# Starting the slabs of the second attention 0.8 ticks later, and the last sums four ticks later

## The chip, the cores and the metric

The kernel runs on one core of a Trainium2 chip. The metric is the device time of one execution in microseconds. The time before is the median of three runs, 2865.06 us (2863.92 to 2869.85). About 0.2% is what such a measurement can tell from no change.

## The reference

The input `x` has 128 graphs of 64 nodes with 768 features, and `adj` is a mask of 64 x 64 for each graph. There are two layers. Each computes an attention over the nodes of a graph under the mask, adds its input and normalises. The first layer (12 heads of 64) takes its scores from tanh of the hidden features, and mixes its result with its input through a gate. The second (6 heads of 128) is ordinary attention with queries, keys, values and an output matrix:

```python
q = _heads(seq_inputs @ Wq + bq)
k = _heads(seq_inputs @ Wk + bk)
v = _heads(seq_inputs @ Wv + bv)
scores = jnp.einsum('bhqd,bhkd->bhqk', q, k) / np.sqrt(HEAD_SIZE)
bias = jnp.where(graph_mask, 0.0, NEG)[:, None]
probs = jax.nn.softmax(scores + bias, axis=-1)
ctx = jnp.einsum('bhqk,bhkd->bhqd', probs, v)
ctx = ctx.transpose(0, 2, 1, 3).reshape(seq_inputs.shape[0], seq_inputs.shape[1], H)
return ctx @ Wf + bf
```

All is float32. The change touches only the second layer.

## The kernel before

The 8192 tokens are 64 tiles of 128 tokens (two graphs each). The first phase treats them in pairs of tiles and ends by about 1440 us. The second treats them in 16 quads of four tiles. Matrix products are made by schemes with fewer multiplications: a product of 2 x 2 blocks takes 7 products of sums of blocks (`TURNS`), and the output matrix, 2 x 3 blocks by 3 x 3, takes 15 (`FIFTEEN`). TensorE therefore waits for sums that VectorE (DVE) or GpSimd (POOL) make, and its results are read out by DVE or ScalarE (ACT).

A quad runs through three steps, f = 0, 1, 2, each for two heads (f and f + 3). A step has these parts:

- `queries` and `keys`: seven products each, in `by_feature` (L442). The readers of their results are given by `p1` to `p7`: P1 and P2 go to ACT (L422 and L425), the others to DVE (L418, L428, L431, L434). The results stand in `zone`, in one buffer for queries and one for keys. The five PSUM banks of the pool `dense` are used in turn by all these products.
- `slab(Q, f)`: the scores (`s_ps`, L991), with mask and maximum on DVE (L1001, L1005), subtraction (L1007), exponential on ACT (L1009), sum and division on DVE (L1012 to L1016). Then the weights are turned: ACT sorts them into halves (L1030), SP issues a transposing DMA (L1031), ACT sorts them back in two copies (L1035). TensorE multiplies them with the values (`c_ps`, L1047). ACT copies this out in two halves (L1061), two transposing DMAs follow on SP (L1062), and four ACT copies (L1069) put the result into `cT`. In the last quad's f = 2, TensorE turns the weights and no DMA is used. Just after `c_ps` of f = 2, the mask and the values of the next quad are loaded (`load`: L970, and eight DMAs at L980).
- `output(before, i)`, at f = 1 and f = 2: the 15 products (L1135) for two tiles (i = 0, then 1) of the quad before. DVE adds each result to a row tile `y` (L1148).

The sums of the output's scheme are made by `operands` (L1102 on DVE; in the last quad's second pair also L1100 on POOL). Rows are loaded by `rows_of` (L1113 on SP, then POOL adds a bias, L1118), and `normed` closes a tile: statistics on DVE (L363 to L368), a power on POOL (L370, L371), the scaling on ACT (L1161) and the store on SP (L1163). There are four `y` buffers; a load into one waits until the store from it has landed. In the keys of f = 2, each operand block of the next quad is loaded as soon as its product has been issued (L397).

Every engine executes its instructions in the order in which the program issues them. That order is written by `Beat`, a clock that exists only while the program is built. A query, key or value product advances it by one tick, an output product by 2/3. `start` puts a line of steps (a generator) on this clock: its first step comes `after + 0.7` ticks from now, and each `yield n` puts the next step n ticks later. The reader of a product comes 1.5 ticks after it. Nothing waits for ticks on the chip: they decide only what stands before what in each engine's queue.

```python
def step(time):
    wait = next(line, None)
    if wait is not None:
        self.at(time + wait, lambda: step(time + wait), order)
time = self.now + after + 0.7
self.at(time, lambda: step(time), order)
```

The slab of a step is started when its keys have been issued. Its scores thus come 1.7 ticks after the keys, `c_ps` 12 ticks after the scores, the first copies into `cT` 18 and the second 19 ticks after them. Since 2/3 is added many times over, steps whose times nearly agree can change places from one quad to the next.

After the last quad, `output` runs twice more. The sums for its second pair of tiles are started 5 ticks (and 0.7) after those of the first.

Of the kernel before, what the change touches and what calls it, by code (L numbers as in the profile page):

```python
# [208 lines left out]
def two_layers(  # L209
# [23 lines left out]
    n_quads = n_tiles // 4  # L233
    n_pairs = n_tiles // 2
    beat = Beat()
# [5 lines left out]
    def sb(pool, shape, tag, name, bufs=None, dtype=F32):  # L241
        return pool.tile(shape, dtype, tag=tag, name=name, bufs=bufs)
# [140 lines left out]
    def in_zone(at, *shape):  # L383
        size = math.prod(shape)
        letters = " ".join("abc"[: len(shape)])
        sizes = dict(zip("abc", shape))
        return zone[:, at : at + size].rearrange(f"p ({letters}) -> p {letters}", **sizes)
# [4 lines left out]
    def load_block(q, k):  # L392

        at = PLACES[k] * KH
        t = in_zone(IN_ZONE[k] * D, KH, 2, P)
        for i in range(2):
            nc.sync.dma_start(t[:, :, i, :], ops_there[q][:, i, at : at + KH, :])  # L397
        return t.rearrange("p c i t -> p c (i t)")

    def queries(q, f, blocks, part):  # L400
        quads[q]["qT"] = in_zone(7 * KH * 2 * P, 2, 4 * P)
        by_feature(f"q_{q}_{f}_", blocks, ready["wq_sb"], f, bq_sb, quads[q]["qT"], part)

    def keys(q, f, blocks, part, then=None):
        quads[q]["kT"] = in_zone((7 * KH + 4) * 2 * P, 2, 4 * P)
        by_feature(f"k_{q}_{f}_", blocks, ready["wk_sb"], f, bk_sb, quads[q]["kT"], part, then)
# [500 lines left out]
    def phase_b(pb, ps_b):  # L907
# [166 lines left out]
        def operands(Q, i):  # L1074

            while not Q.get("done"):
                yield 1
            c = Q["c"][i]
            A = [c[:, :, k, m] for m in range(2) for k in range(3)]

            last = Q["q"] + 1 == n_quads and i == 1
            s = in_zone(0, 11, 2, P) if last else sb(pb, [P, 11, 2, P], "sc", f"sc_{Q['q']}_{i}", 1)
            of = Q["ob", i] = {f"A{k}": a for k, a in enumerate(A)}
            sums = (
                ("3", 1.0, "A0", "A2", ALU.subtract),
                ("12", -1.0, "3", "A3", ALU.subtract),
                ("2", 1.0, "A5", "A4", ALU.subtract),
                ("11", 1.0, "2", "3", ALU.subtract),
                ("14", 1.0, "A0", "A3", ALU.add),
                ("7", -1.0, "A1", "A3", ALU.subtract),  # L1090
                ("0", 1.0, "A1", "A4", ALU.add),
                ("10", 1.0, "0", "A5", ALU.subtract),
                ("5", 1.0, "A0", "A1", ALU.subtract),
                ("1", 1.0, "10", "A2", ALU.subtract),
                ("6", 1.0, "A3", "A4", ALU.subtract),
            )
            for k, (name, sign, a, b, op) in enumerate(sums):
                of[name] = s[:, k]
                if last and sign == 1.0:
                    nc.gpsimd.tensor_tensor(s[:, k], of[a], of[b], op)  # L1100
                else:
                    nc.vector.scalar_tensor_tensor(s[:, k], of[a], sign, of[b], ALU.mult, op)  # L1102
                yield 1

        def rows_of(Q, i):
            q = Q["q"]

            while "bias" not in ready or q and not all(quads[q - 1].get(("out", i, k)) for k in range(2)):
                yield 1
            for k in range(2):  # L1110
                t = 4 * q + 2 * k + i
                y = sb(pb, [P, D], "y", f"y_{t}", 4)
                nc.sync.dma_start(y, x1_there[t])  # L1113
                Q["y", i, k] = y
            yield 2
            for k in range(2):
                y = Q["y", i, k]
                nc.gpsimd.tensor_tensor(y, y, bf_sb, ALU.add)  # L1118
                yield 1

        def output(Q, i):
            q, of = Q["q"], Q["ob", i]
            y = [Q["y", i, k] for k in range(2)]
            sums = {}
            left = [sum(b // 3 == k for *_, to in FIFTEEN for _, b in to) for k in range(2)]
            for at, xb, wb, to in FIFTEEN:
                beat.until(lambda: xb in of)
                begun = at in sums
                if not begun:
                    sums[at] = sb(dense[0], [P, BANK], "dense", f"o_{q}_{i}_{at}")[:, 0:THIRD]  # L1130
                ps = sums[at]

                def emit():
                    for c in range(2):
                        nc.tensor.matmul(  # L1135
                            ps,
                            lhsT=of[xb][:, c, :],
                            rhs=wf_sb[:, wb, c, :],
                            start=(c == 0 and not begun),
                            stop=(c == 1),  # L1140
                            skip_group_check=True,
                        )

                def read(ps=ps, to=to):
                    for sign, b in to:
                        k, n = divmod(b, 3)
                        part_of = y[k][:, n * THIRD : (n + 1) * THIRD]
                        nc.vector.tensor_tensor(part_of, part_of, ps, ALU.add if sign > 0 else ALU.subtract)  # L1148
                        left[k] -= 1
                        if not left[k]:  # L1150
                            beat.start(normed(y[k], 4 * q + 2 * k + i), 0)

                beat.product(emit, read, 2 / 3)
# [12 lines left out]
        Q, before = quads[0], None  # L1166

        def at_place(q, f):

            return (None, 0, 1)[f]  # L1170

        load(Q)
        for q in range(n_quads + 1):
            for f in range(3):
                if f == 2 and q < n_quads:
                    beat.start(rows_of(Q, 0))
                if f == 0 and before:
                    beat.start(rows_of(before, 1))
                if before and at_place(q, f) is not None and (q < n_quads or f == 1):
                    beat.start(operands(before, at_place(q, f)))  # L1180
                    if q == n_quads and f == 1:
                        beat.start(operands(before, 1), 5)
                if q < n_quads and (q or f):
                    queries(q, f, blocks, part)
                if q < n_quads:
                    then = None
                    if f == 2 and q + 1 < n_quads:
                        then = lambda xb: blocks.update({xb: load_block(q + 1, xb)})
                    if q or f:
                        keys(q, f, blocks, part, then)  # L1190
                    beat.start(slab(Q, f), 1)
                i = at_place(q, f)
                if before and i is not None:
                    beat.until(lambda: ("ob", i) in before)
                    output(before, i)
            before, Q = Q, quads.get(q + 1)
        beat.drain()

    with (
        tc.tile_pool(name="pb", bufs=1) as pb,  # L1200
        tc.tile_pool(name="ps_b", bufs=1, space=PSUM) as ps_b,
        tc.tile_pool(name="dense_b", bufs=5, space=PSUM) as dense_b,
        tc.manual_schedule(),
    ):
        dense[:] = [dense_b]
        phase_b(pb, ps_b)
# [47 lines left out]
```

## Time and profile before

| what | value |
|---|---|
| median of three runs | 2865.06 us |
| the profiled execution, its own time | 2868.3 us |
| its span | 2866.4 us |
| granted TensorE clock, mean | 0.994 |
| TensorE busy | 2804.1 us, 98% of the span |
| VectorE busy | 2039.1 us, 71% |
| ScalarE busy | 1305.3 us, 46% |
| GpSimd busy | 1067.2 us, 37% |
| first scores of the second layer | 1441.8 us |
| last c_ps turned by DMA | 2792.85 us |

The profiled execution runs about 2 us longer than its span, and about 3 us longer than the median. In the views below, a row of waits names the engine and line that waited, and what it waited for, with the total, the number of times and the longest. A row of the timeline has its start, its length, the engine, the line, the instruction and how many were merged; `[t <- X]` is idle time ahead of it and what ended it. SPq is the queue of SP, and its time is that of issuing a DMA, including what it waits for in the course of that, not that of the transfer. In a table of windows the third last number is the granted TensorE clock, followed by the share of the DMA engines and GB/s.

### The profile page before, as it was taken

Reading aid. Unit: us, or ns where it says so; the run is one execution under the profiler, and the core shown is the slowest. Engines: PE = TensorE matmul, PEld = TensorE weight load, DVE = VectorE, ACT = ScalarE, POOL = GpSimd, SP = SyncE. Lnnn points to the kernel's source line nnn. Section 1 sums busy time; section 2 is a strip of 40 time slices with the busy share of each in tenths; the row PEclk is TensorE's granted clock in tenths of the full one; section 3 lists DMA queues with packets and bytes.
Section 4 is the critical chain, followed back from the end, with each engine's and each line's share of the span. In section 5 each row is a group of like instructions: output and inputs, shape, how many; then the busy total and the mean of one; then the engine's idle time right before and its main releaser. Section 6 shows DMA issues by size and latency. Waiting matters only on the chain.

```text
span 2866.4 us, 43840 instructions
## 1 busy us (share of the span) xinstructions
PE 2804.1 (98%) x16168; PEld 2038.1 (71%) x16168; DVE 2039.1 (71%) x4103; ACT 1305.3 (46%) x1562; POOL 1067.2 (37%) x938
## 2 busy tenths in 40 slices
PE   7899999999999999999899999999999999999998
PEld 4455555555555555555588888888888888888886
DVE  6888888888888888888636555565555655556556
ACT  2655655665665665665423333333333333333331
POOL 6656656666665665665421101101011110110102
PEclk9999999999999999999999999999999999999999
DMA  6666666666666666667764445534355343554532
GB/s 205 152 175 170 175 168 169 179 165 170 182 163 172 179 165 170 186 160 193 195 156 116 106 100 131 135 87 117 86 130 135 90 120 84 127 135 94 128 82 63
DMA packets 627014, 409.61 MB, mean 143 GB/s; under 512 B 440176, under 2 KB 573040, under 8 KB 626800
## 3 DMA queue, kind: packets, MB, share of 16 engines
q1 hardware_dynamic: 626800, 406.81, 55.2%
q8 instruction: 128, 2.10, 0.3%
q14 instruction: 86, 0.70, 0.1%
HBM read 186.69 MB, written 119.93 MB: 107 GB/s over the span
## 4 chain that ended last, share of the span: by engine, by line
PE 89%; DMA 4%; DVE 2%; SPq 1%; ACT 1%; issue 1%; POOL 0%; POOLq 0%; ACTq 0%; DVEq 0%
PE v L346 15%; PE o L1135 15%; PE h L346 14%; PE g L346 14%; PE q L442 14%; PE k L442 12%; PE f_all L742 2%; PE s_ps L991 2%; PE c_ps L1047 2%; DMA out<-y 2%; DMA sT<-parts 2%; SPq L980 1%; ACT cT L1069 0%; PE bias_ps L951 0%; DMA s<-parts 0%
## 5 line engine op out<-in xcount | busy, mean ns | idle before, releaser
L370 POOL TENSOR_TENSOR rs<-rs,power 128x1 f32<-128x1 f32 x128 | 73.9, 577 | 1079.4 <-DVE rs L368 1079.4
L346 PE MATMUL h<-w,zone 128*128 128x384 f32 x1320 | 446.2, 494 | 21.7 <-ACT h L533 12.5
L442 PE MATMUL q<-zone,w 128*128 128x256 f32 x2016 | 461.6, 384 | 3.8 <-issue 1.2
L346 PE MATMUL g<-w,zone 128*128 128x384 f32 x1320 | 441.3, 489 | 4.4 <-DVE gate L587 3.3
L442 PE MATMUL k<-zone,w 128*128 128x256 f32 x2016 | 443.2, 379 | 0.9 <-ACT k_u L422 0.9
L442 PEld LDWEIGHTS q<-zone,w 128*128 128x128 f32 x2016 | 381.2, 191 | 63.5 <-issue 8.4
L442 PEld LDWEIGHTS k<-zone,w 128*128 128x128 f32 x2016 | 382.9, 190 | 53.4 <-ACT k_u L422 1.3
L346 PEld LDWEIGHTS h<-w,zone 128*128 128x128 f32 x1320 | 250.7, 192 | 194.6 <-ACT h L533 13.7
L346 PEld LDWEIGHTS g<-w,zone 128*128 128x128 f32 x1320 | 247.5, 190 | 176.4 <-DVE gate L587 12.8
L1135 PE MATMUL o<-w,sc 128*128 128x256 f32 x1364 | 326.7, 384 | 4.7 <-DVE sc L1102 4.7
L1148 DVE TENSOR_TENSOR y<-y,o 128x256 f32<-128x256 f32 x512 | 206.7, 415 | 126.7 <-PE o L1135 120.1
L1135 PEld LDWEIGHTS o<-w,sc 128*128 128x128 f32 x1364 | 256.1, 191 | 43.8 <-DVE sc L1102 6.0
L346 PE MATMUL v<-w,x_sums 128*128 128x384 f32 x768 | 258.5, 486 | 1.7 <-DVE x_sums L315 1.7
L1118 POOL TENSOR_TENSOR y<-y,bf_sb 128x768 f32<-128x768 f32 x64 | 118.4, 1865 | 342.4 <-DMA y<-x_there 313.9
L662 POOL TENSOR_TENSOR bc_e<-th_d,w_dst_sb 128x768 f32<-128x768 f32 x64 | 120.0, 1875 | 287.2 <-ACT th_d L557 267.6
L346 PEld LDWEIGHTS v<-w,x_sums 128*128 128x128 f32 x768 | 145.7, 190 | 104.0 <-DVE x_sums L315 3.0
L1161 ACT ACTIVATE y<-y,rs 128x768 f32<-128x768 f32 x64 | 65.7, 1026 | 157.8 <-POOL rs L371 157.8
L657 POOL TENSOR_SCALAR zone<-zone 128x768 f32<-128x768 f32 x64 | 137.3, 2146 | 0.0
L1009 ACT ACTIVATE s<-s 128x512 f32<-128x512 f32 x48 | 30.1, 626 | 226.2 <-DVE s L1007 226.2
L1102 DVE SCALAR_TENSOR_TENSOR sc<-cT 128x256 f32<-128x256 f32 x217 | 113.9, 525 | 22.9 <-ACT cT L1069 22.8
L650 ACT ACTIVATE gate<-gate 128x768 f32<-128x768 f32 x64 | 53.9, 843 | 166.8 <-DVE gate L593 118.5
L733 ACT COPY bc_e<-th_d 128x1536 uint16<-128x1536 uint16 x64 | 123.2, 1926 | 13.2 <-DMA th_d<-bc_e 13.2
(162 smaller groups left out, 4625.1 us busy)
## 6 DMA issues: line engine op xcount, KB each, us to landing
zone<-ops_there SPq DMA_DIRECT2D x224, 192.0 KB, 4.4
zone<-in_xT SPq DMA_DIRECT2D x32, 768.0 KB, 6.2
zone<-in_x SPq DMA_DIRECT2D x64, 384.0 KB, 3.9
bc_e<-there SPq DMA_DIRECT2D x128, 192.0 KB, 3.4
x_there<-mix SPq DMA_DIRECT2D x64, 384.0 KB, 4.2
ops_there<-x_sums SPq DMA_DIRECT2D x32, 768.0 KB, 3.3
v_there<-v SPq DMA_DIRECT2D x128, 192.0 KB, 2.6
v<-v_there SPq DMA_DIRECT2D x128, 192.0 KB, 3.9
```

The source lines that it names most:

```text
L346: nc.tensor.matmul(ps, lhsT=blocks[xb][:, c, :], rhs=w[:, wb, c, :], start=(c == 0 and to not in begun), stop=(c == KH - 1), skip_group_ch ...
L370: nc.gpsimd.tensor_tensor(rs[:, 0:1], rs[:, 0:1], power, ALU.pow)
L442: nc.tensor.matmul(ps, lhsT=w[:, wb, c, f * P : (f + 1) * P], rhs=blocks[xb][:, c, :], start=(c == 0 and to not in begun), stop=(c == KH - 1),
L657: nc.gpsimd.tensor_scalar(xs, xs, 1.0, None, ALU.add)
L662: nc.gpsimd.tensor_tensor(bc, th, w_dst_sb, ALU.mult)
L733: nc.scalar.copy(halves(e), by_halves(d))
L742: nc.tensor.matmul(f_all[b * N : (b + 1) * N, at : at + E0 + 1], lhsT=e[rows, hd // 2 * P + b * N : hd // 2 * P + (b + 1) * N], rhs=(h[row ...
L1102: nc.vector.scalar_tensor_tensor(s[:, k], of[a], sign, of[b], ALU.mult, op)
L1118: nc.gpsimd.tensor_tensor(y, y, bf_sb, ALU.add)
L1135: nc.tensor.matmul(ps, lhsT=of[xb][:, c, :], rhs=wf_sb[:, wb, c, :], start=(c == 0 and not begun), stop=(c == 1), skip_group_check=True,)
L1148: nc.vector.tensor_tensor(part_of, part_of, ps, ALU.add if sign > 0 else ALU.subtract)
L1161: nc.scalar.activation(y, y, AF.Identity, bias=rs[:, 1:2], scale=rs[:, 0:1])
```

## The change

Two numbers in the loop of the second phase change. The slab of a step starts 1.8 ticks (and 0.7) after its keys have been issued instead of 1; the very last slab (last quad, f = 2) keeps its 1. The sums for the very last pair of tiles start 9 ticks (and 0.7) after instead of 5.

```diff
                 if before and at_place(q, f) is not None and (q < n_quads or f == 1):
                     beat.start(operands(before, at_place(q, f)))
                     if q == n_quads and f == 1:
-                        beat.start(operands(before, 1), 5)
+                        beat.start(operands(before, 1), 9)
                 if q < n_quads and (q or f):
                     queries(q, f, blocks, part)
...
                     if q or f:
                         keys(q, f, blocks, part, then)
-                    beat.start(slab(Q, f), 1)
+                    beat.start(slab(Q, f), 1 if q + 1 == n_quads and f == 2 else 1.8)
```

No instruction is added or removed. What changes is the place of a slab's steps among the products and their readers in the queues of TensorE, DVE, ACT and SP, and of the last sums in those of DVE and POOL.

## The prediction

> **What bounds the kernel now.** I read the page first, then the waits of TensorE from 1350 us on (the second attention), then the chain that ended last, then SP's and ACT's timelines around its bends.
>
> ```profile
> PE 2804.1 (98%) x16168; PEld 2038.1 (71%) x16168; DVE 2039.1 (71%) x4103; ACT 1305.3 (46%) x1562; POOL 1067.2 (37%) x938
> ```
>
> TensorE is busy in 98% of the span, and the change adds and removes no matmul. It can only alter the idle 62 us, and the clock. The waits in the second attention:
>
> ```profile
> engine line waited for: us in total, times, longest us
> PE s_ps L991 <- ACT zone L425: 9.3, 11, 2.2
> ...
> PE o L1135 <- DVE sc L1102: 4.7, 3, 2.1
> ```
>
> All eleven 9.3 us stand at the scores of f=0, once a group of four tiles: 0.47 us at 1689, then 1.24, 2.22, 0.33, 0.31, 0.91, 0.40, 0.79, 0.91, 0.47, 1.23 from 1955 to 2755. The chain shows what is late in the last of them:
>
> ```profile
> 2743.85 0.33 ACT k_u L422
> 2744.18 4.19 DMA out<-y
> ...
> 2748.84 4.71 DMA sT<-parts
> ...
> 2754.26 0.75 ACT cT L1069
> 2755.01 0.34 ACT zone L425
> ...
> 2755.39 1.15 PE s_ps L991 x32
> ```
>
> Read upwards: the scores need a key block that ACT finishes at L425; ahead of L425 in ACT's order stand the copies L1069 of the previous group's f=2 slab; they need its second transpose; that stands on SP behind a load of y, which waits until a store of out has landed and freed its buffer. The same stretch of SP, in this late group and in an early one:
>
> ```profile
> 2737.84 6.25 SPq L980 DMA_DIRECT2D v<-v_there  x8
> 2744.18 0.55 SPq L1163 DMA_DIRECT2D out<-y  x1
> 2744.81 1.39 SPq L1062 DMA_TRANSPOSE s<-parts  x1
> 2746.25 2.49 SPq L1113 DMA_DIRECT2D y<-x_there  x2
> 2748.84 1.24 SPq L1062 DMA_TRANSPOSE sT<-parts  x1
> ```
> ```profile
> 1585.10 5.19 SPq L980 DMA_DIRECT2D v<-v_there  x8
> 1590.35 1.07 SPq L1113 DMA_DIRECT2D y<-x_there  x2
> 1591.51 1.27 SPq L1062 DMA_TRANSPOSE s<-parts  x1
> 1592.87 3.34 SPq L1062 DMA_TRANSPOSE sT<-parts  x1
> ```
>
> Early groups (quads 1 to 4) store both out tiles before the v loads, so their y loads wait for nothing (1.07 us, not 2.49); from quad 5 on the order is the other one. This gives a natural measure. From one f=2 c_ps (L1047) to the next the timeline has 88.07, 88.61, 88.06 and 88.08 us early; later 89.14, 91.79, 88.22, 88.20. From 1584.21 to 2737.33 are 13 periods in 1153.12 us; at 88.06 they would take 1144.78. The excess is 8.34 us, and the last wait (1.23) comes after it: 9.57 us in all.
>
> [...] alone (L1031 at 2764.42) its reader starts 4.39 us later; behind v and y loads (1591.51) 5.84. [...] after the 2.22 us wait the granted clock is 0.50 in 2047 to 2049, which is why that period lost 3.7; and in the tail:
>
> ```profile
> 2826.00:2828.00 2.00, 2.00 (x6) 1.57 (x5) 1.46 (x6) 0.03 (x1) 0.98 (x3) 0.50 0.50 197
> ```
>
> [...] sums at L1102 take 0.42, but 1.76 at 2835.20 while POOL runs L1118, and 0.94 and 0.96 beside POOL's L1100.
>
> **The change, part by part.** (1) The later start moves every step of a slab 0.8 ticks down. A product is one tick, 6 matmul records or 1.29 us (7 take 9.06); an output product is 0.86. In the built order the scores of f=0 stand after three products of the next queries, not two; c_ps of f=2 after five, not four; c_ps of f=0 after the first output product, not before it; scores of f=1 and f=2 after four output products, not three. Count of instructions, DMAs and bytes is the same.
>
> (2) SP's order from quad 5 on becomes the early one in every group: out, out, mask, eight v, two y, two transposes. Behind f=1 both y loads also go ahead of both transposes, as quads 1 to 5 have them today; the zone loads follow either way 9.0 to 9.3 us after the first out store.
>
> (3) What late groups then wait: c_ps f=2 and the scores shift by the same 1.29 us, so twelve products still lie between (16.77 us when undisturbed). L425 must begin 0.51 before the scores. In the early order it begins 15.66, 16.79, 16.02 and 15.31 us after c_ps: slack 0.60, -0.53, 0.24, 0.95. In the late order 17.58, 18.54, 16.65, 16.64, 17.24. In quads 1 to 5 of the changed kernel L425 also passes ahead of the second pair of copies (1.27 us less), so no wait; in quads 6 to 14 it does not, and one in four of the early order's sizes would wait 0.54: 9 x 0.13 = 1.2 us remain. So -9.6 + 1.2 = -8.4.
>
> (4) Covers of the moved steps. The product that now precedes the scores needs a PSUM bank last read by DVE (third product of the keys, read at 2750.3, needed at 2754.2): hidden. The weights' copy before f=0's c_ps: L1030 moves behind the next k_u on ACT (ready 2764.9 in the old clock), transpose 4.4, two copies 1.4: ready 2771.9, c_ps due at 2773.1: 1.2 us slack (2.0 today). For f=1 and f=2 a y normalisation (1.03) now stands between the two weight copies of L1035; today both end 1.0 to 1.2 before c_ps. In f=1 the second copy would end at 2793.5, its half of c_ps due at 2794.6: 1.1 slack. Early groups already run this order (1581.65, 1582.62, 1583.55 on ACT) with a c_ps that does not wait. Queued behind these copies are L425 of the queries, due 6 us later at the bank, and the c_ps reads. Cost 0; if the slack were gone, each tenth of a us would count 45 times. Bounds: -1 to +3 us.
>
> (5) The tail: sums of the last pair start four ticks later. DVE's one at 2836.88 ("12" of the last pair, 0.94 long) goes behind "6" of the pair before; POOL's first ("3") goes behind both L1118. TensorE's 2.10 us wait at 2839.43 ends with DVE's "10", which began at 2838.41. Without the 0.94 it would start about 2837.6 and last 0.96 again, as POOL now does three sums there: product "10" at 2838.6, 0.8 us earlier. POOL's remaining sums, behind the powers at 2845.4 and 2847.5, run to about 2852 at 0.73 each; "14" is needed at 2850.8, "10" at 2852.4, "6" at 2855.8: covered. The 1.73 and 0.90 waits before stay, and the half clock with them. -0.8, bounds -1.5 to +1.5.
>
> Sum: -8.4 + 0 - 0.8 = -9.2. The profiled execution took 2868.3 (span 2866.4); it becomes 2859.1. The median of the three is 2865.06, 3.2 below it; taking the same difference from that: 2855.9.
>
> **The rivals.** *A: the wait stays under a new name.* With the y loads (768 KB) ahead of both, the first transpose lands later (13.1, 14.3, 12.9, 12.8 us after c_ps early, against 11.1 to 12.5 in late groups); if late groups sit where the 14.3 sits, each of nine waits 0.54 and the clock now and then halves. For: the second quad did. Against: three of four have slack. Then 9.6 - 4.9 + 0.8 saved less one clock loss of 1.5: 2861.
>
> *B: nothing.* The waits of 0.3 to 1.2 in late groups depend on where DMA landings fall (out stores also load the queues); shifted by the same 1.29 as their consumer they keep their size, and only the tail's 0.8 is saved: 2864. Against: the order that delays the second transpose is gone from every group.
>
> *C, slower: the weights' copies become the bound.* The y normalisation between the two L1035 copies waits for a power from POOL; in early groups ACT waits 4.1 us for one of these. If it comes more than 1.1 us late at f=1 or f=2, c_ps waits, 30 times. At 0.6 us each, 18 us lost, less 9: 2874. It decides from 1.1 us of lateness; the row of L370 waits for DVE's sums of squares, whose place beside the output products does not move. Against it also the early groups.
>
> *D: the tail starves.* If POOL's sums ran at the 0.8 to 0.95 they take beside DVE, "10" would be 0.5 late at most; inside the bounds.
>
> **How the numbers follow.** Forecast (2852 to 2859): 0.62. A: 0.14. B: 0.13. C: 0.11. Bounds of parts 4 and 5, and a spread of the before's own runs of 1 below to 5 above their median, widen the forecast to 2850; A and B are taken in up to 2865; C is left out. About 0.2% (5.7 us, so 2859.3) is what a measurement here tells from no change: the forecast and a third of A are beyond it, so faster 0.69 after a little for the forecast's own upper edge and parts of A; within: the rest of A and B and a few of the forecast, 0.20; slower 0.11.
>
> **What would show it.** In the changed kernel's waits "s_ps <- ACT zone" should fall from 9.3 to about 1 us; periods between f=2 c_ps should be 88.0 to 88.6 throughout; on SP no y load after v should take over 1.5 us; L425 should begin 15.3 to 16.8 after c_ps; TensorE's last "o <- DVE sc" wait should be about 1.3, not 2.1. The forecast is wrong if c_ps shows waits for ACT L1035 or L1161, if the bank of the third product waits, or if periods keep 88.3 or more.

## The result, and the profile after

The changed kernel takes 2859.33 us (median of 8 runs, 2854.74 to 2859.91) against 2868.86 us for the kernel before, run beside it (8 runs, 2863.88 to 2873.95). The ratio is 0.9962, with a 95% interval of 0.9952 to 0.9971: faster by 9.5 us. The prediction was a fall of 9.2 us, to 2855.9 from a median of 2865.06; the kernel before, run again, lies 3.8 us above that median, so it is the falls that compare. The profiled execution of the changed kernel took 2859.59 us, with a span of 2857.3; before, 2868.3 and 2866.4.

The page of the changed kernel, engines:

```profile
PE 2803.1 (98%) x16168; PEld 2039.0 (71%) x16168; DVE 2042.6 (71%) x4103; ACT 1309.1 (46%) x1562; POOL 1063.8 (37%) x938
```

TensorE's busy time is 1.0 us less than it was (2804.1). So 8.1 of the 9.1 us of span are idle time that has gone. TensorE's waits in the second attention of the changed kernel (total, times, longest):

```profile
engine line waited for: us in total, times, longest us
...
PE o L1135 <- DVE sc L1102: 5.0, 3, 2.3
...
PE s_ps L991 <- ACT zone L425: 1.5, 3, 0.6
...
PE q L442 <- DVE zone L428: 1.2, 1, 1.2
PE q L442 <- ACT q_u L422: 1.0, 1, 1.0
```

The wait of the scores has fallen from 9.3 us in 11 places to 1.5 us in 3 (0.63 at 1953.60, 0.53 at 2481.22, 0.33 at 2746.57). Two names are new at this size: the next queries wait once for DVE's L428 and once for ACT's L422. The wait in the tail is no shorter.

SP's timeline of the changed kernel, in the late group that answers to the one at 2737 before:

```profile
2725.40 2.49 SPq L1163 DMA_DIRECT2D out<-y  x2
2727.95 0.42 SPq L970 DMA_DIRECT2D a8b<-in_adj  x1
2729.90 5.62 SPq L980 DMA_DIRECT2D v<-v_there  x8
2735.58 1.06 SPq L1113 DMA_DIRECT2D y<-x_there  x2
2736.74 1.28 SPq L1062 DMA_TRANSPOSE s<-parts  x1
2738.11 4.28 SPq L1062 DMA_TRANSPOSE sT<-parts  x1
```

Both stores now stand ahead of the mask and the v loads. The y loads behind v take 1.06 us to issue, where they took 2.49 while they waited for a store. The transposes follow each other directly. The chain that ended last, at the same place in the changed kernel:

```profile
2736.74 6.78 DMA s<-parts
...
2743.54 0.91 ACT cT L1069 x2
...
2744.81 1.38 ACT cT L1069 x2
2746.19 0.33 ACT zone L425
...
2746.57 1.15 PE s_ps L991 x32
```

The store, the y load and the second transpose are no longer in it. What is late is the first transpose, now behind v and y, and then the four copies and L425 on ACT. From `c_ps` of f = 2 (2729.39) to L425 (2746.06) are 16.67 us, and a wait of 0.33 is left.

From one `c_ps` of f = 2 to the next the changed kernel takes 87.82 to 87.91 us in nine of 13 periods, and 88.43, 88.52, 89.15 and 89.26 in the other four. From 1583.43 to 2729.39 are 13 periods in 1145.96 us, against 1153.12 before: 7.16 us. The last wait of the scores fell from 1.23 to 0.33: 0.90 more. The rest of the span's 9.10 us is made up so: 1.38 us less up to the first query product (1412.56 before, 1411.18 after), where the change touches nothing; 0.69 less in the first quads, not traced; and 1.03 more in the tail and behind it (30.40 us before and 31.36 after from the start of the first product behind the 1.73 wait to the start of the last products, and 0.07 to the span's end).

### The profile page after: what moved, and what is told of

Read it like the earlier page. It is cut to its first block, busy times and chain, and to the rows that moved or that the text cites. A ratio compares the mean times of both kernels' runs of the same rounds, so it can differ in the third digit from the quotient of the medians.

```text
span 2857.3 us, 43775 instructions
## 1 busy us (share of the span) xinstructions
PE 2803.1 (98%) x16168; PEld 2039.0 (71%) x16168; DVE 2042.6 (71%) x4103; ACT 1309.1 (46%) x1562; POOL 1063.8 (37%) x938
## 4 chain that ended last, share of the span: by engine, by line
PE 90%; DMA 2%; DVE 2%; ACT 1%; issue 1%; SPq 1%; POOL 0%; POOLq 0%; DVEq 0%; ACTq 0%
PE o L1135 15%; PE q L442 14%; PE v L346 14%; PE h L346 14%; PE k L442 14%; PE g L346 14%; PE f_all L742 2%; PE s_ps L991 2%; PE c_ps L1047 2%; DMA s<-parts 1%; DMA th_d<-bc_e 0%; DMA elu_turned<-xg_parts 0%; DMA sT<-parts 0%; PE bias_ps L951 0%; DMA ops_there<-x_even 0%
## 5 line engine op out<-in xcount | busy, mean ns | idle before, releaser
L1135 PE MATMUL o<-w,sc 128*128 128x256 f32 x1364 | 317.3, 381 | 5.0 <-DVE sc L1102 5.0
L1118 POOL TENSOR_TENSOR y<-y,bf_sb 128x768 f32<-128x768 f32 x64 | 117.2, 1841 | 314.3 <-DMA y<-x_there 290.8
L1102 DVE SCALAR_TENSOR_TENSOR sc<-cT 128x256 f32<-128x256 f32 x217 | 116.6, 537 | 32.4 <-ACT cT L1069 32.4
L1061 ACT COPY parts<-c_ps 128x1024 uint16<-128x1024 uint16 x94 | 90.6, 1015 | 106.2 <-PE c_ps L1047 106.2
L1135 PE MATMUL o<-w,cT 128*128 128x256 f32 x512 | 132.6, 392 | 0.0
```

Of the source, the lines that this page charges most:

```text
L1061: nc.scalar.copy(by_halves(parts), halves(c_ps[:, r].rearrange("p i t -> p (i t)")))
L1135: nc.tensor.matmul(ps, lhsT=of[xb][:, c, :], rhs=wf_sb[:, wb, c, :], start=(c == 0 and not begun), stop=(c == 1), skip_group_check=True,)
```

## The experiments

All are edits of the kernel before, timed in five rounds against it on one chip for each group of three or four. In the table, *nine late periods* is the time from `c_ps` of f = 2 in quad 5 to that in quad 14, in the profiled execution. The shortest period that recurs in these traces takes 87.82 us, so nine of them 790.4; that is called the floor. The column on SP says whether both stores of out stand ahead of v at f = 2 from quad 5 on. The column on slack says how many products later the scores of f = 0 come than before, counted from `c_ps` of f = 2. Waits and periods are those of one execution each.

| kernel | stores first | slack | waits of the scores, us (times) | nine late periods, us | ratio, 95% interval |
|---|---|---|---|---|---|
| before | no | 0 | 9.3 (11) | 800.30 | 1 |
| changed kernel | yes | 0 | 1.5 (3) | 793.26 | 0.9962 (0.9952 to 0.9971) |
| slabs only | yes | 0 | 1.8 (3) | 793.19 | 0.9968 (0.9956 to 0.9980) |
| sums only | no | 0 | 11.1 (10) | 800.35 | 0.9994 (0.9986 to 1.0002) |
| f = 0 only | no | +1 | 0.6 (1) | 790.44 | 0.9958 (0.9946 to 0.9971) |
| f = 2 only | yes | -1 | 13.2 (9) | 808.24 | 1.0010 (1.0002 to 1.0017) |
| f = 1 only | no | 0 | 11.8 (13) | 798.81 | 0.9991 (0.9984 to 0.9998) |
| f = 0 and f = 1 | no | +1 | 1.3 (3) | 791.46 | 0.9963 (0.9949 to 0.9977) |
| stores first, late groups | yes | 0 | 8.2 (10), 2.4 (6) in late groups | 793.02 | 0.9975 (0.9966 to 0.9984) |
| stores first, all groups | yes | 0 | 2.7 (4) | 794.40 | 1.0055 (1.0043 to 1.0068) |
| f = 0, and stores first in all | yes | +1 | none listed | 790.40 | 1.0041 (1.0027 to 1.0054) |
| f = 0 and sums | no | +1 | 0.4 (1) | 790.50 | 0.9958 (0.9945 to 0.9970) |
| f = 0 at 2.6 | no | +2 | none listed | 795.69 | 0.9987 (0.9979 to 0.9995) |

### The two halves of the change

The slabs alone:

```diff
-                    beat.start(slab(Q, f), 1)
+                    beat.start(slab(Q, f), 1 if q + 1 == n_quads and f == 2 else 1.8)
```

> The kernel before with the slabs' start alone moved (1.8; the last sums stay at 5). All theories that put the gain at the scores of f=0: TensorE's wait of L991 for L425 falls from 9.3 us to the 1.5 us of the changed kernel, median 8 to 10 us under before. Theory 'the last sums cost time': the stretch from the first output product of the last quad to the end of the span is 40.9 us as before, not the 41.9 of the changed kernel, so this kernel is about 1 us faster than the changed one. Rival 'the later sums gain 0.8 us and the half clock took it back': the stretch varies with the clock by 1 to 2 us whatever the sums do.

The sums of the last pair alone:

```diff
-                        beat.start(operands(before, 1), 5)
+                        beat.start(operands(before, 1), 9)
```

> The kernel before with the last sums alone moved (9 instead of 5). Waits at the scores of f=0 stay at about 9.3 us. My forecast's step 5: TensorE's wait before output product '10' falls from 2.1 to about 1.3 us and the time by 0.8 us. Rival: POOL's bias additions stretch the sums of DVE ahead of '10', so the wait stays at 2.1 to 2.4 us and the time is unchanged within 0.5 us, or up to 2 us more where the clock halves after it.

The slabs alone gave 2858.57 us against 2867.18 (0.9968), the sums alone 2867.08 (0.9994, an interval that holds 1). The slabs carry the gain. What the sums are worth lies within what can be measured.

### The scores' deadline, or SP's order

The slabs do two things at f = 2 and f = 0: they put SP into the other order, and they move two ends of the same stretch. The move of f = 0 gives the scores one product more; the move of f = 2 takes it away again and changes SP's order. These two runs take the two apart.

```diff
-                    beat.start(slab(Q, f), 1)
+                    beat.start(slab(Q, f), 1.8 if f == 0 else 1)
```

> The kernel before with only the slabs of f=0 started at 1.8. The late quads keep the order store, mask, eight v, store, transpose, two y, transpose on SP, and the scores of f=0 come one product (1.29 us) later. Theory 'deadline': each of the eleven waits shrinks by 1.29 us, leaving about 0.9 us in one of them, so 8 to 9 us faster. Theory 'order on SP': the second transpose is as late as before because of the y load that waits for a store; the waits stay near 9 us and nothing is gained.

```diff
-                    beat.start(slab(Q, f), 1)
+                    beat.start(slab(Q, f), 1.8 if f == 2 and q + 1 < n_quads else 1)
```

> The kernel before with only the slabs of f=2 started at 1.8 (not the very last). The late quads get the early order on SP (both stores, mask, eight v, two y, two transposes), but c_ps of f=2 comes 1.29 us later while the scores of f=0 stay where they were. Theory 'order on SP' alone: waits fall to 1 to 2 us, 8 us faster. By my slack of 0.60, -0.53, 0.24, 0.95 us for the early order, less 1.29 us: nine late quads wait 0.3 to 1.8 us each, 9 us in all, so no gain (within 2 us of before).

The waits of the scores, with f = 0 alone moved:

```profile
PE s_ps L991 <- ACT zone L425: 0.6, 1, 0.6
```

And with f = 2 alone:

```profile
PE s_ps L991 <- ACT zone L425: 13.2, 9, 2.3
```

With f = 0 alone the order on SP is the old one, and L425 begins 16.65 to 17.63 us after `c_ps` from quad 6 on, as late as before (16.64 to 18.54 there). But the scores come 1.29 us later, and nothing waits: the late periods are at their floor, and the whole gain is there (2855.12 us, 0.9958). With f = 2 alone SP's order is the new one, but the scores have 1.29 us less: the waits grew, and the kernel is no faster (2869.43 us, 1.001). This profiled execution was 7 us above the kernel's median; so its waits are above what is usual.

For f = 1 alone, which moves neither end (it puts the y loads ahead of both transposes behind f = 1 in the late groups too):

```diff
-                    beat.start(slab(Q, f), 1)
+                    beat.start(slab(Q, f), 1.8 if f == 1 else 1)
```

> Slabs of f=1 alone begin at 1.8, those of f=0 and f=2 stay at 1. Deadline theory: the scores of f=0, the only ones that wait, do not move, nor does c_ps of f=2; the waits stay at 9 to 11 us, the ratio 0.999 to 1.001. If any later slab loosens ACT or SP for the others, the waits fall below 6 us and the ratio below 0.998.

It gave 2866.18 us against 2868.38 (0.9991), with waits of 11.8 us. It differs from before in the early periods: 87.83 us for the first, 88.07 before. In quad 2 the 0.24 lies between `c_ps` of f = 1 and that of f = 2: 32.30 us here and 33.84 before, of which the move itself takes 1.3. The rest is `c_ps` of f = 1 itself. In the early quads before, it takes 1.35 us, not 1.10:

```profile
1638.44 1.35 PE L1047 MATMUL c_ps<-v,sT 64*64 64x128 f32 x32
```
```profile
1637.39 1.03 ACT L1161 ACTIVATE y<-y,rs 128x768 f32<-128x768 f32 x1 [0.54 <-POOL rs L371]
1638.32 0.76 ACT L1035 COPY sT<-s 128x512 uint16<-128x512 uint16 x1
```

Its second half starts at 1639.13, when the second weights' copy ends (1639.08); that copy stands on ACT behind a scaling that waits for POOL. With f = 1 one product later, `c_ps` takes 1.10 us there, and so it does in the changed kernel.

### SP's order by itself

The normalised tiles start 0.1 ticks earlier, so that both stores come ahead of the mask and v; no slab is moved.

```diff
-                            beat.start(normed(y[k], 4 * q + 2 * k + i), 0)
+                            beat.start(normed(y[k], 4 * q + 2 * k + i), -0.1)
```

> The kernel before with one number changed: the normalised out tiles start 0.1 ticks ahead of where they stood, so that SP stores both of them before the v loads in every group, as the early groups do; no slab is moved. Deadline theory (the late f=0 scores gain one product of slack): the slack of the scores is unchanged; by the early order's sizes (0.60, -0.53, 0.24 and 0.95 us against c_ps f=2) the waits fall from 11 us to about 2 us in nine late groups, the gain is about 7 us, ratio 0.9975. Order theory (SP's order is what matters): the same gain or more, because the second transpose no longer stands behind a y load that waits for a store. If the order matters little, as the run that moved f=2 alone hints, waits stay at 6 to 11 us and the ratio at 0.999 to 1.

This was slower by 15 us (2882.96 against 2868.38). The waits of TensorE in the second attention, and the timelines of SP, of DVE and of TensorE in quad 1 show why:

```profile
PE q L442 <- DVE zone L428: 19.5, 5, 5.0
```
```profile
1580.20 2.50 SPq L1163 DMA_DIRECT2D out<-y  x2
1582.80 2.88 SPq L1113 DMA_DIRECT2D y<-x_there  x2
1585.73 0.42 SPq L970 DMA_DIRECT2D a8b<-in_adj  x1
```
```profile
1589.48 1.87 DVE L972 TENSOR_SCALAR biasb<-a8b 128x256 f32<-128x256 uint8 x1 [7.35 <-DMA a8b<-in_adj]
```
```profile
1591.80 1.65 PE L442 MATMUL q<-zone,w 128*128 128x256 f32 x3 [5.01 <-DVE zone L428]
```

In the four early groups the edit also moved the y loads, ahead of the mask. They wait for the stores (2.88 us to issue, where the changed kernel's take 1.06) and move 768 KB; the mask, issued behind them at 1585.73, lands late; DVE stands at L972 for 7.35 us, to 1589.48; L428, queued behind it, is what frees the bank of a query product; and TensorE waits 5.01, 3.86, 4.46 and 5.01 us in the four groups. The mean granted clock of this execution was 0.99, against 0.994 before. The nine late groups, where y stays behind v, took 794.40 us, 5.9 less than before. The edit was not the one that was wanted, so it was made again for the late groups alone:

```diff
-                            beat.start(normed(y[k], 4 * q + 2 * k + i), 0)
+                            beat.start(normed(y[k], 4 * q + 2 * k + i), -0.1 if q >= 4 else 0)
```

> The order of SP alone, cleanly: both out tiles are stored ahead of the v loads and the y loads behind them from quad 5 on, as the changed kernel has it, and the four early groups stay as they are; no slab is moved. In the earlier run with the same edit in all groups, the y loads also passed ahead of the mask in the four early groups, which cost TensorE 3.9 to 5.0 us of waiting each; its nine late groups took 794.4 us against 800.3 before. Deadline and order theory together: waits at the scores fall from 11 us to 2 to 3.5 us, the gain is 5 to 7 us, ratio 0.9975 to 0.998. If the order is worth nothing by itself: 1.000.

It gave 2859.92 us against 2867.46: 0.9975, a gain of 7.2 us by the ratio. The nine late periods took 793.02 us, as good as the changed kernel's (793.26). So the order with both stores first is worth 7 us where the ends stay at their distance. SP's order in the late groups is the changed kernel's, behind f = 1 too. The edit moves two things more, both ahead of `c_ps` of f = 2: the scaling L1161 goes between the two weights' copies on ACT, as it does in the changed kernel, and one of the sums L1102 on DVE goes behind the first statistics. They were not separated from SP's order; with f = 1 alone, where SP's order behind f = 1 and the scaling there move likewise, the waits stayed at 11.8 us.

The profiled execution is this kernel's longest (2865.30 us): the four early groups, in which the order on no engine differs from before, waited 0.60, 1.20, 1.61 and 2.37 us, because the first transpose landed later (below).

Both together, and with the sums:

```diff
-                            beat.start(normed(y[k], 4 * q + 2 * k + i), 0)
+                            beat.start(normed(y[k], 4 * q + 2 * k + i), -0.1)
...
-                    beat.start(slab(Q, f), 1)
+                    beat.start(slab(Q, f), 1.8 if f == 0 else 1)
```

> Slabs of f=0 alone at 1.8, and both out tiles stored before the v loads in every group. Deadline theory: the run with f=0 alone left 0.6 us of waits at the scores, so at most that is to be had: ratio 0.9955 to 0.996. If the mask load, which now stands behind two stores, brings back the waits of the queries for DVE's zone read that the changed kernel shows (1.17 us once), it is that much slower: 0.9963.

```diff
-                        beat.start(operands(before, 1), 5)
+                        beat.start(operands(before, 1), 9)
...
-                    beat.start(slab(Q, f), 1)
+                    beat.start(slab(Q, f), 1.8 if f == 0 else 1)
```

> Slabs of f=0 alone at 1.8, and the sums of the very last pair at 9, not 5. Deadline theory: as f=0 alone (0.9958) plus what the sums are worth. Moving the sums alone gave 0.9994, and the difference between the two kernels with all slabs moved is within 1 us either way; so 0.9950 to 0.9964. If the sums' move mattered by more than 1 us, it would show here as below 0.995 or above 0.997.

The first carries the same early fault (2880.31 us); in the nine late periods it has 790.40 us, as f = 0 alone has (790.44). Once the deadline is moved, SP's order is worth nothing more in the late groups. With the sums it is 2855.75 us, 0.9958, as without them.

### What the full change loses against f = 0 alone

The changed kernel's nine late periods are 2.9 us above the floor. Which of the two other moves costs that:

```diff
-                    beat.start(slab(Q, f), 1)
+                    beat.start(slab(Q, f), 1.8 if f < 2 else 1)
```

> Slabs of f=0 and f=1 at 1.8, those of f=2 stay at 1: the changed kernel's slabs without the move of f=2. Deadline theory: as f=0 alone, 0.9958 (waits under 1 us at the scores, none for DVE's zone read behind the mask, since the mask stays ahead of the second store). If the 2 to 3 us by which the full change falls behind f=0 alone came from f=1's move, 0.9967.

It gave 2856.49 us (0.9963), with 791.46 us in the nine late periods; no wait for L428 appears, and the mask stays ahead of the second store. In these single traces, then, the move of f = 2 costs about 2 us (793.26 us with the full change, 793.19 with all slabs moved and the sums left). The ratios of this run and of the slabs alone (0.9963 and 0.9968) do not tell them apart. A small part of it is at the scores, whose waits in these periods come to 1.17 us with the full change, 1.83 with the slabs alone, 0.92 in this run. The largest single part is one wait of a query product, in the changed kernel's timelines of DVE and TensorE:

```profile
2555.29 0.29 DVE L972 TENSOR_SCALAR biasb<-a8b 128x256 f32<-128x256 uint8 x1 [5.08 <-DMA a8b<-in_adj]
2555.50 0.48 DVE L428 SCALAR_TENSOR_TENSOR zone<-q,bq_sb,q_u 128x256 f32<-128x256 f32 x1
```
```profile
2556.03 1.56 PE L442 MATMUL q<-zone,w 128*128 128x256 f32 x6 [1.17 <-DVE zone L428]
```

The mask is now issued behind the second store. DVE waited 0.65 us for it in a late group before (at 2117.84) and waits 2.8 us or more now. At 2555 the mask landed 4.44 us after its issue, where 2.2 is usual; DVE waited 5.08 us, and L428 was late for TensorE. Before, a mask that landed as late (4.06 us, read at 2028) made DVE wait 2.56 us and TensorE not at all. With the slabs alone DVE's longest such wait in a late group is 4.34 us, and no wait for L428 is listed.

Later still, for f = 0 alone:

```diff
-                    beat.start(slab(Q, f), 1)
+                    beat.start(slab(Q, f), 2.6 if f == 0 else 1)
```

> Slabs of f=0 at 2.6 in place of 1, the others at 1: one more product of slack at the scores of f=0. With 1.8 only 0.6 us of waits was left, so the deadline theory gives at most that: 0.9955 to 0.9960. If the softmax behind the scores, or its first transpose, has less cover than it seems, new waits at c_ps f=0 appear and the ratio rises above 0.997.

```profile
PE q L442 <- ACT q_u L422: 3.1, 4, 1.5
```

2863.12 us, 0.9987: most of the gain is gone. The scores no longer wait, but the fourth query product, which now stands ahead of them, waits in four places for a bank, whose reader L422 stands on ACT behind the copies L1069 and L425 (1.50 us at 2045.89, where L422 begins at 2045.48). The same late transpose has found another waiter. In quads where no wait is listed a period still takes 88.14 us (2116.17 to 2204.31), 0.32 above the floor. There a query product starts 0.22 us late for DVE's L428 (2139.52, where L428 ends at 2139.47), which now stands behind the softmax steps L1001 to L1007 on DVE. Of the three starts tried for f = 0 (1, 1.8 and 2.6), 1.8 is the best. That kernel is as fast as the changed one, and no run here shows it to be faster: 0.9958 and 0.9962 have intervals that overlap almost wholly.

## Why the prediction was right, and where it was not

**Step 1 and 2, the moves.** SP's order became the early one in every group, as said, and no y load behind v took over 1.5 us (1.06 or 1.07 in every quad).

**Step 3, the waits of late groups.** The mechanism is shown. That SP's order gives the gain while both ends move by the same 1.29 us is what the run with the stores first in late groups shows (7.2 us with neither end moved), and the runs with f = 0 and f = 2 alone show the 1.29 us of each end. The size was nearly right too: -8.4 predicted, -7.16 - 0.90 = -8.06 found. But the terms of that sum were off. The undisturbed period is 87.82 us, not 88.06, which was read off early groups; these were slow by 0.24 because `c_ps` of f = 1 waited for its second weights' copy. 13 x 0.24 = 3.1 us were therefore missing from the excess before (12.7 us, not 9.57), and the excess that remains is 4.6 us (1145.96 - 13 x 87.82 = 4.30, and 0.33), not 1.2. The early order's four sizes gave the scores' share of it fairly: 1.5 us. The other part is the two new waits (1.17 and 1.03), and some 0.9 in no listed wait. So 3.1 us too little before and 3.4 us too little after nearly cancel, and that the sum came out close is luck. The span's whole fall of 9.1 us agrees with 9.2 by more luck: 2.07 us of it came from ahead of the first full period, which the prediction left out, and the tail took 1.03 back.

**Step 4, the covers.** The weights' copies did not become the bound: no `c_ps` waits for L1035 or L1161 in the changed kernel, so rival C is out. Its kind of wait did exist, in the kernel before: the step took the early groups for proof that a scaling between the two copies costs nothing, which holds at f = 2; at f = 1 it cost 0.25 us in each of them, and the move of f = 1 took that away. And the list of what was moved past what was incomplete. The mask is a DMA on SP, and it moved behind the second store; behind its reader L972 on DVE stands L428, for which TensorE's next product waits. The step asked what was queued behind the moved instructions on ACT, and did not ask it for DVE. The faulty edit shows the price of that cover when it is gone: 3.9 to 5.0 us in each group. Here it cost 1.17 us once, inside the bound of 3.

**Step 5, the tail.** The term itself came true; that it would show in the time did not. The last wait is 2.34 us, not 1.3, and the stretch is 0.96 us longer, inside the bounds of 1.5. TensorE before, and in the changed kernel:

```profile
2839.43 2.00 PE L1135 MATMUL o<-w,sc 128*128 128x256 f32 x8 [2.10 <-DVE sc L1102]
```
```profile
2828.61 2.70 PE L1135 MATMUL o<-w,sc 128*128 128x256 f32 x8 [2.34 <-DVE sc L1102]
```

In the table all times count from the start of the stretch, the first product behind the 1.73 wait. The last column is the stretch from product "10" on.

| kernel | sums at | product "10" starts, us | its wait, us | clock falls behind it | from there, us |
|---|---|---|---|---|---|
| before | 5 | 13.94 | 2.10 | no | 16.46 |
| f = 0 only | 5 | 13.99 | 2.16 | no | 16.46 |
| slabs only | 5 | 13.99 | 2.98 | yes | 18.13 |
| f = 2 only | 5 | 13.97 | 2.89 | yes | 18.14 |
| f = 0 at 2.6 | 5 | 14.08 | 3.06 | yes | 18.13 |
| sums only | 9 | 13.21 | 2.19 | no | 16.43 |
| changed kernel | 9 | 13.25 | 2.34 | yes | 18.11 |
| f = 0 and sums | 9 | 13.25 | 2.22 | yes | 18.12 |

With the sums later, "10" starts 0.7 to 0.9 us earlier in all three kernels, as forecast. What the step had wrong is the clock, which it held fixed. At the start of the stretch the granted clock was 0.50 for 6.8 us before and for 3.4 with the change, so the product ahead of "10" ended sooner (at 10.9 us against 11.8), and the wait is no shorter although it ends sooner. That is not what moved "10": with the slabs alone the clock was low for 3.4 us too, and "10" starts at 13.99. And behind the wait the clock fell again in the changed kernel and not before; the stretch from "10" on is 1.65 us longer. In this row of the changed kernel the granted clock is third from last:

```profile
2830.00:2832.00 2.00, 2.00 (x7) 1.56 (x6) 1.19 (x4) 0.00 (x0) 0.00 (x0) 0.50 0.00 0
```

Between kernels whose clock does the same behind "10", the later sums are worth 0.76 us (30.40 and 29.64 us for the whole stretch, 32.12 and 31.36). So the size was right, and its loss in this execution is the clock's. With f = 0 and f = 1 moved, "10" starts at 14.01 too, and the clock stays low for 6.8 us behind it; with f = 1 alone the clock did not fall at the start, DVE's sums passed ahead of POOL's additions, and "10" starts at 11.51. The three kernels whose stores were moved have another order in the tail.

The sum of 0.94 us left DVE's queue, as said. Both sums ahead of it met one of POOL's additions (L1118, 2822.64 and 2824.92, 1.8 us each) in the changed kernel:

```profile
2823.18 1.55 DVE L1102 SCALAR_TENSOR_TENSOR sc<-cT 128x256 f32<-128x256 f32 x1
...
2824.99 2.01 DVE L1102 SCALAR_TENSOR_TENSOR sc<-cT 128x256 f32<-128x256 f32 x1
```

Before, the first took 0.70 us and the second 1.76. The step reckoned with such a lengthening for one sum of the two. The longer first sum cost little: the second ends 11.64 us from the start of the stretch, where it ended at 11.48 before.

**The rivals.** A came true in a small part: the waits that are left at the scores, 1.5 us, stand behind the first transpose, as it said, and 2.2 us more stand under two names that it did not give. B is refuted by the waits of the scores, which fell from 9.3 to 1.5 us, and by the run with the stores first in late groups. C is refuted by the absence of its wait, D by product "10", which came sooner.

## What to carry to other kernels

A stretch between two fixed points in the order has two ends and a content: ask of a change which of the three it moves. Here one line of the diff moved both ends alike and changed the content, and moving one end alone (f = 0, one product later) did as much. When an instruction on a DMA queue is moved past another, follow every consumer of both, up to what is queued behind that consumer on its own engine: the mask is a small load, and putting it behind the y loads cost 3.9 to 5.0 us a group. And before a gain of under 2 us is read off one execution, see whether TensorE's clock did the same on both sides: in the tail here, the stretch behind one wait took 18.11 us where the clock fell and 16.46 where it did not.

## What was not expected of the hardware

Under one order of issue a transposing DMA landed at different times. In quad 3 the kernel before and the run with the stores first in late groups have the same order on every engine. Before, the first transpose is issued at 1768.55 and ACT, which waits for it, starts at 1773.80, 5.25 us later; in the other run 1769.24 and 1776.73, 7.49 us later. The two differ by 2.24 us, so by the author's estimate a single trace sizes such a wait to a us or two a group at best. Executions of one kernel differ by some us (2863.88 to 2873.95 before); how much of that comes from such landings was not measured.

The length of TensorE's wait did not tell by itself whether the granted clock fell. Before, the clock was 0.50 from 2826 to 2830, behind the wait of 1.73 us at the start of the tail, and 1.00 from 2838 to 2844, around and behind the longer wait of 2.10 us that ended at 2839.43. In the changed kernel it was 0.50 from 2830 to 2832, behind the wait of 2.34 us that ended at 2828.61. What made the difference was not shown.
